# Edge counting in groups of 125 edges and 12 targets, four groups to a PSUM bank

## The chip, the cores and the metric

The kernel runs on one core of a Trainium2 chip. The metric is the device time of one execution in microseconds (us); the median of the runs is compared. A core has five engines that work side by side, each with a queue of its own: TensorE (PE, with its weight loads shown apart as PEld), VectorE (DVE), ScalarE (ACT), GpSimd (POOL) and SyncE (SP, which issues most DMAs).

## The reference

The input is `x` (1250 tokens by 1024) and a list of 40,000 edges `src`, `dst`, sorted by `dst`. Two layers of a graph network, then a mixture of experts:

```python
def _sage_layer(h, edge_src, edge_dst, deg_inv, W_self, W_neigh, b):
    msg = h[edge_src]
    agg = jax.ops.segment_sum(msg, edge_dst, num_segments=h.shape[0])
    mean = agg * deg_inv[:, None]
    return h @ W_self + mean @ W_neigh + b
...
h = jax.nn.relu(_sage_layer(x, ..., W_self0, W_neigh0, b0))
out = _sage_layer(h, ..., W_self1, W_neigh1, b1)
...
x = x + gnn(layernorm(x), src, dst, ...)
x = x + ffn(layernorm(x), ...)     # router, two of eight experts a token
```

All in float32. The targets are drawn so that low numbers get many more edges than high ones: `dst` is 1250 times the square of a uniform number.

## The kernel before

The kernel doesn't gather messages. It builds a matrix `C` of counts once (source by target, 10 blocks of 128 sources by 1250 targets) and multiplies with it: the sum over the edges becomes a product, in both layers.

**How counts are made.** The edges, in order of target, are cut into groups of 250 (`EG`), each of two chunks of 125 (`GC`, `GP`). Two groups make a row of groups; there are `R` = 80 rows. The targets of a group lie close together, so the group counts into a window of `WIN` = 24 targets that begins at its own base. A source number is taken apart into a high part (its block, 0 to 9) and a low part (its lane, 0 to 127). For each chunk `row_of_groups` makes two one-hot matrices in float16: `ol` on POOL (L409, edge by lane, 128 wide) and `oh` on DVE (L416, edge by block and window place, `NB * WIN` = 240 wide). A matmul of the two (L419) counts the edges of the chunk by lane, block and window place, and the two chunks of a group add up in PSUM. The two groups of a row share one PSUM bank (`cnt`, three buffers).

**How they get into `C`.** Two rows of groups are left open. Then `close_row` takes the oldest: for each of its groups it loads the base from SBUF into a register of DVE (`values_load`, L433) and adds the window to `C` at this place (L438, 128 x 240 float32). `oh` and `ol` have six buffers each (pool `hot`).

**What comes ahead of it.** `make_keys` works out, for every edge, its place in the window (block times `WIN` plus target minus base) and its lane, with edges in rows of 500; `turn_keys` brings them into the layout of one edge a partition by transposes, and `turn_ranges` the bases and the least and greatest target of each group into one row. `verdict` tests on DVE whether every group fits its window. If not (`plain` is 0), the kernel runs a general path at its end. The general path isn't run for these inputs.

**What the order is.** The first steps are in an order written by hand (L467 to L495). After that the instructions are placed by the scheduler of the framework, by program order and by its estimate of when each is ready; on each engine the order is then fixed. The program mixes the rows of groups with the products of the first layer: 9 rows around the first of them, then 10 rows for each 128 columns of the rest of `W_self0` (`self_unit`, L458, two or four rows to a unit), then one row to each of the ten `y_unit`s of the first quarter of `W_neigh0` (L524), and the last row after these. When all rows are closed, a product with ones sums `C` over the sources (L549) and gives the degrees; then the first product with `C` follows (L560). So nothing after L549 can begin before the last add of L438. The rest of the kernel (second layer, router, experts) doesn't touch what is changed here.

Of the kernel before, what the change touches and what calls it, by code (L numbers as in the profile page):

```python
# [10 lines left out]
F32 = mybir.dt.float32  # L11
F32R = mybir.dt.float32r
F16 = mybir.dt.float16
# [3 lines left out]
ALU = mybir.AluOpType  # L17
AX = mybir.AxisListType
# [2 lines left out]

P = 128
EPS = 1e-5
WIN = 24
GC, GP = 2, 125


@with_exitstack
def kernel(
# [21 lines left out]
    nc = tc.nc  # L51
    N, D = x.shape
    NE = src.shape[0]
# [4 lines left out]
    QW = D // 4  # L58
    NB = -(-N // P)
    NP = NB * P  # L60
    EG = GC * GP
    NGR = NE // EG
    R = NGR // 2
    WEXP = KD * H + KH * D
    NTILE = (2 * N) // P + E
    assert R * 2 * EG == NE and R <= P and 2 * NB * WIN <= 512 and N > WIN
    rows = [min(P, N - b * P) for b in range(NB)]

    step = -(-(N - 2 * P) // 4) * 2
# [3 lines left out]
    def blk(b):  # L73
        return slice(b * P, b * P + rows[b])
# [4 lines left out]
    const = ctx.enter_context(tc.tile_pool(name="const", bufs=1))  # L79
# [11 lines left out]
    L = land.tile([P, NT + 4 * D + 2 * WQ], F32, name="L")  # L91
# [4 lines left out]
    def row_of(i):  # L96
        return SC[:, (i % 4) * D : (i % 4 + 1) * D]
# [7 lines left out]
    def load_q(w, q):  # L105

        t = WW[:, turn[0] * WQ : (turn[0] + 1) * WQ].rearrange("p (k n) -> p k n", k=KD)
        turn[0] ^= 1
        tc.keep_in_program_order(
            nc.sync.dma_start(  # L110
                out=t, in_=w[:, q * QW : (q + 1) * QW].rearrange("(k p) n -> p k n", p=P)
            )
        )
        return t
# [27 lines left out]
    stt = nc.vector.scalar_tensor_tensor  # L142


    RE = 2 * EG
    assert 8 * RE <= 4000 and 3 * NGR <= 500 and 8480 + 6 * NGR <= 9440
    edge = L[:R, 4000:8000].rearrange("p (a n) -> p a n", n=RE)
    dst_i, src_i, hi_i, lo_i = (edge[:, a, :].bitcast(I32) for a in range(4))
    dst_f, hi_f, lo_f, key = (edge[:, a, :] for a in range(4, 8))
    for b in range(2):  # L150
        for h, eng in enumerate((nc.sync, nc.scalar)):
            hs = slice(h * HALF, (h + 1) * HALF)
            eng.dma_start(out=row_of(b)[: rows[b], hs], in_=x[blk(b), hs])
    nc.sync.dma_start(out=dst_i, in_=dst.rearrange("(g n) -> g n", n=RE))
    nc.scalar.dma_start(out=src_i, in_=src.rearrange("(g n) -> g n", n=RE))
    ws_first = load_q(w_self0, 0)
# [9 lines left out]
    ident = const.tile([P, P], F32, name="ident")  # L166
# [22 lines left out]
    lane = counted(iota([P, P], [[1, P]]), "lane", F16)  # L189
# [6 lines left out]
    nc.scalar.dma_start(out=b0_p, in_=b0.rearrange("(k p) -> p k", p=P))  # L196


    ext = const.tile([R, 3, 2], F32, name="ext")
    base_i = const.tile([1, NGR], I32, name="base_i")  # L200

    keys = const.tile([GP, 2, 2 * GC, R], F32, name="keys")
    worst = const.tile([1, 1], F32, name="worst")
    plain = const.tile([1, 1], I32, name="plain")
    gx = L[:1, 8000 : 8000 + 3 * NGR].rearrange("o (a g) -> o a g", a=3)
    lo_, hi_ = gx[:, 0, :], gx[:, 1, :]
    APART = 16
    assert APART * EG < 4096

    dst_halves = dst_f.rearrange("p (a n) -> p a n", a=2)  # L210

    def make_keys():

        nc.vector.tensor_reduce(ext[:, 0, :], dst_halves, AX.X, ALU.min)
        nc.vector.tensor_scalar(ext[:, 2, :], ext[:, 0, :], float(N - WIN), None, op0=ALU.min)
        nc.vector.tensor_scalar(hi_i, src_i, 7, None, op0=ALU.arith_shift_right)
        nc.vector.tensor_scalar(lo_i, src_i, P - 1, None, op0=ALU.bitwise_and)
        nc.vector.tensor_copy(hi_f, hi_i)
        nc.vector.tensor_copy(lo_f, lo_i)
        stt(key, hi_f, float(WIN), dst_f, op0=ALU.mult, op1=ALU.add)  # L220
        for i in range(2):
            part = key[:, i * EG : (i + 1) * EG]
            nc.vector.tensor_scalar(part, part, ext[:, 2, i : i + 1], None, op0=ALU.subtract)

    def turn_keys():
        for a, v in enumerate((key, lo_f)):
            ps = tpp.tile([P, 4, P], F32, name="tp")
            pf = ps.rearrange("p a b -> p (a b)")
            for c in range(2 * GC):
                nc.tensor.transpose(  # L230
                    pf[:GP, c * R : (c + 1) * R], v[:, c * GP : (c + 1) * GP], ident[:R, :R]
                )
            nc.scalar.copy(keys[:, a].rearrange("p c g -> p (c g)"), pf[:GP, : 2 * GC * R])

    def turn_ranges():

        nc.vector.tensor_reduce(ext[:, 1, :], dst_halves, AX.X, ALU.max)
        for a in (2, 0, 1):
            pe = tpp.tile([P, 4, P], F32, name="tp")
            for i in range(2):  # L240
                nc.tensor.transpose(pe[:1, i, :R], ext[:, a, i : i + 1], ident[:R, :R])
            nc.vector.tensor_copy(
                gx[:, a, :].rearrange("o (r i) -> o i r", i=2), pe[:1, :2, :R]
            )
            if a == 2:
                nc.vector.tensor_copy(base_i, gx[:, 2, :])

    def verdict():

        bad = L[:1, 8480 : 8480 + 6 * NGR].rearrange("o (a g) -> o a g", a=6)  # L250
        nc.vector.memset(bad, -1.0)
        stt(bad[:, 0, :], hi_, float(1 - WIN), lo_, op0=ALU.add, op1=ALU.subtract)
        nc.vector.tensor_tensor(bad[:, 1, : NGR - 1], lo_[:, : NGR - 1], lo_[:, 1:], ALU.subtract)
        nc.vector.tensor_tensor(bad[:, 2, : NGR - 1], hi_[:, : NGR - 1], hi_[:, 1:], ALU.subtract)
        stt(
            bad[:, 3, : NGR - APART], hi_[:, : NGR - APART], 1.0, lo_[:, APART:],
            op0=ALU.add, op1=ALU.subtract,
        )
        nc.vector.tensor_scalar(bad[:, 4, :], hi_, float(1 - N), None, op0=ALU.add)
        nc.vector.tensor_scalar(bad[:, 5, :], lo_, -1.0, None, op0=ALU.mult)  # L260
        nc.vector.tensor_reduce(worst, bad.rearrange("o a g -> o (a g)"), AX.X, ALU.max)
        nc.vector.tensor_scalar(plain, worst, 0.0, None, op0=ALU.is_le)
# [90 lines left out]
    def gnn_windows():  # L353
# [6 lines left out]
        pc = pcs.enter_context(tc.tile_pool(name="pc", bufs=3, space=PSUM))  # L360
# [18 lines left out]
        hot = y0.enter_context(tc.tile_pool(name="hot", bufs=6, side="right"))  # L379

        yh = yp.tile([P, NB, QW], F32R, name="yh")
        yl = yp.tile([P, NB, QW], F32R, name="yl")
        win = yp.tile([P, NB * WIN], F16, name="win")
        win_i = yp.tile([P, NB * WIN], I32, name="win_i")
        nc.gpsimd.iota(win_i, pattern=[[1, NB * WIN]], base=0, channel_multiplier=0)
# [18 lines left out]
        GW = NB * WIN  # L404

        def row_of_groups(r):
            ol = hot.tile([GP, 2 * GC, P], F16, name="ol")
            for c in range(2 * GC):
                nc.gpsimd.tensor_scalar(  # L409
                    ol[:, c, :], lane[:GP], keys[:, 1, c, r : r + 1], None, op0=ALU.is_equal  # L410
                )
            ps = pc.tile([P, 2, 256], F32, name="cnt")
            for i in range(2):
                for c in range(GC):
                    oh = hot.tile([GP, GW], F16, name="oh")
                    nc.vector.tensor_scalar(  # L416
                        oh, win[:GP], keys[:, 0, i * GC + c, r : r + 1], None, op0=ALU.is_equal
                    )
                    nc.tensor.matmul(  # L419
                        ps[:, i, :GW], ol[:, i * GC + c, :], oh,  # L420
                        start=(c == 0), stop=(c == GC - 1),
                    )
            open_rows.append((r, ps))
            if len(open_rows) > 2:
                close_row()
# [2 lines left out]

        def close_row():
            r, ps = open_rows.pop(0)  # L430
            for i in range(2):
                g = 2 * r + i
                at = nc.values_load(  # L433
                    base_i[0:1, g : g + 1], engines=(ENG.DVE,), min_val=0, max_val=N - WIN,
                    skip_runtime_bounds_check_because="cut at N - WIN, and a target is never below 0",
                )
                to = C[:, :, ds(at, WIN)]
                nc.vector.tensor_tensor(  # L438
                    to, to.bitcast(F32),
                    ps[:, i, :GW].rearrange("p (k w) -> p k w", k=NB), ALU.add,  # L440
                )
# [64 lines left out]
        some_groups(2)  # L506
        self_unit(ws_first, 1, 2)
        verdict()
        for q in range(1, 4):
            w_q = w_next  # L510
# [21 lines left out]
        for q in range(4):  # L532
# [8 lines left out]
            if q == 0:  # L541
# [4 lines left out]
                for c0, n in cchunks:  # L546
                    ps = mm.tile([P, 512], F32, name="ps")
                    for k in range(NB):
                        nc.tensor.matmul(  # L549
                            ps[:, :n], ones_r, C[:, k, c0 : c0 + n],  # L550
                            start=(k == 0), stop=(k == NB - 1),
# [3 lines left out]
            for c0, n in cchunks:  # L555
                for d in (2 * q, 2 * q + 1):
                    ps = mm.tile([P, 512], F32, name="ps")
                    for k in range(NB):
                        for part in (yh, yl):
# [3 lines left out]
                                start=(k == 0 and part is yh), stop=(k == NB - 1 and part is yl),  # L563
# [1093 lines left out]
```

## Time and profile before

| | us |
|---|---|
| three runs | 1163.17, 1163.0, 1160.78 |
| median | 1163.0 |
| the profiled execution, its own time | 1160.5 |
| its span, first to last instruction | 1158.6 |
| first one-hot on POOL (L409) | 32.2 |
| last add into `C` (L438) begins | 234.2 |
| column sums (L549) begin | 234.6 |

The mean granted TensorE clock is 0.993. Times in the profile are counted from the first instruction of the span. In a line of a group stand the source line, engine, operation, what it writes and reads, the shape and the number of instructions; then their busy time in us, the mean of one in ns, and the idle time of the engine just before them with what ended it. In the table by stages each engine has its busy time and the number of instructions; the last three columns are the granted clock, the share of DMA and GB/s. `DVEq` is DVE's sequencer, which loads registers and works out addresses; its instructions count as no busy time.

### The profile page before, as it was taken

How to read it: one execution, taken by the hardware profiler on the slowest of the kernel's cores; microseconds unless marked ns; L12 is line 12 of the kernel's file. 1: busy time of each engine (PE TensorE's matmuls, PEld its weight loads, DVE VectorE, ACT ScalarE, POOL GpSimd, SP SyncE). 2: the span in 40 equal slices, each digit the busy share in tenths (PEclk: the TensorE clock that was granted, in tenths of full speed). 3: DMA queues.
4: the chain of work that ended last, by engine and by line, in shares of the span. 5: the costliest groups of instructions: out<-in, count | busy, mean ns of one | idle time of the engine just before them, and what ended most of it. 6: DMA issues, size and time to landing. Idle time of an engine off the chain costs nothing.

```text
span 1158.6 us, 13209 instructions
## 1 busy us (share of the span) xinstructions
PE 1122.4 (97%) x4775; PEld 789.3 (68%) x4775; DVE 452.2 (39%) x1127; ACT 181.5 (16%) x420; POOL 331.3 (29%) x438
## 2 busy tenths in 40 slices
PE   6999999999999999999999999999999989999994
PEld 4556556888888886887788688865333666666662
DVE  8767778751212164241234142555221532111110
ACT  5301000001111111100110000122111223222220
POOL 1899999700000000031004011540000013323221
PEclk9999999999999999999999999999999999999997
DMA  7011011010100021042014432347801435554542
GB/s 230 32 40 39 1 37 37 1 37 1 37 1 1 1 73 37 10 170 72 1 34 164 167 118 73 145 164 257 279 19 36 146 89 132 107 121 101 126 116 45
DMA packets 59330, 95.40 MB, mean 82 GB/s; under 512 B 8797, under 2 KB 35645, under 8 KB 59251
## 3 DMA queue, kind: packets, MB, share of 16 engines
q1 hardware_dynamic: 48400, 67.72, 17.0%
q0 software_dynamic: 7056, 23.88, 9.1%
q10 hardware_dynamic: 3798, 2.84, 0.8%
q8 instruction: 42, 0.69, 0.2%
q14 instruction: 34, 0.28, 0.1%
HBM read 68.76 MB, written 27.47 MB: 83 GB/s over the span
## 4 chain that ended last, share of the span: by engine, by line
PE 94%; DVE 2%; ACT 1%; DMA 1%; POOL 1%; issue 0%; ACTq 0%; DVEq 0%; POOLq 0%
PE ps L524 12%; PE ps L458 11%; PE psb L638 9%; PE ps L708 8%; PE ps L560 8%; PE ps L638 7%; PE ps L1493 7%; PE ps L1518 7%; PE ps L1173 5%; PE ps L625 5%; PE ps L1186 4%; PE cnt L419 3%; PE ps L1128 2%; PE tp L1481 2%; PE lg L1105 2%; PE ps L1514 1%
## 5 line engine op out<-in xcount | busy, mean ns | idle before, releaser
L409 POOL TENSOR_SCALAR ol<-lane,keys 125x128 f16<-125x128 f16 x320 | 192.1, 619 | 27.7 <-DVE oh L416 27.7
L458 PE MATMUL ps<-h0T,L 128*128 128x498 f32 (+2 forms) x384 | 147.6, 517 | 0.3 <-ACT h0T L321 0.2
L524 PE MATMUL ps<-L,h0T 128*128 128x256 f32 (+1 forms) x640 | 142.2, 379 | 0.0
L704 POOL TENSOR_TENSOR L<-L 128x512 f32<-128x512 f32 (+1 forms) x20 | 32.0, 1608 | 375.6 <-DVE L L617 217.6
L524 PEld LDWEIGHTS ps<-L,h0T 128*128 128x128 f32 (+1 forms) x640 | 118.3, 187 | 18.0 <-issue 0.6
L416 DVE TENSOR_SCALAR oh<-win,keys 125x240 f16<-125x240 f16 x320 | 85.7, 322 | 30.9 <-PE cnt L419 29.1
L458 PEld LDWEIGHTS ps<-h0T,L 128*128 128x128 f32 x384 | 67.5, 192 | 39.0 <-issue 33.9
L1493 PE MATMUL ps<-xw,L 128*128 x368 | 84.7, 383 | 0.3 <-issue 0.3
L1518 PE MATMUL ps<-xw,L 128*128 x184 | 83.5, 596 | 0.1
L560 PE MATMUL ps<-C,yh 128*128 128x256 f32 (+2 forms) x240 | 81.8, 356 | 0.0
L560 PE MATMUL ps<-C,yl 128*128 128x256 f32 (+2 forms) x240 | 81.5, 353 | 0.0
L708 PE MATMUL ps<-zh,C 128*128 128x512 f32 (+1 forms) x200 | 79.5, 398 | 0.0
L708 PE MATMUL ps<-zl,C 128*128 128x512 f32 (+1 forms) x200 | 78.6, 393 | 0.0
L1493 PEld LDWEIGHTS ps<-xw,L 128*128 128x128 f32 x368 | 69.0, 192 | 10.1 <-issue 1.4
L1529 POOL DMA_INDIRECT out_dram<-L x23 | 36.3, 1579 | 133.4 <-ACT L L1482 87.9
L1470 POOL DMA_INDIRECT L<-t_d,L x26 | 26.0, 1000 | 162.2 <-DVE L L140 142.2
L438 DVE TENSOR_TENSOR C<-C,cnt 128x240 f32 x160 | 64.4, 402 | 13.4 <-DVE oh L416 2.1
L1518 PEld LDWEIGHTS ps<-xw,L 128*128 128x128 f32 x184 | 33.2, 190 | 35.3 <-issue 33.0
L140 DVE TENSOR_TENSOR L<-L,ps 128x512 f32<-128x512 f32 (+1 forms) x28 | 17.1, 611 | 99.7 <-PE ps L1173 47.2
L419 PEld LDWEIGHTS <-ol 125*128 125x128 f16 x320 | 31.0, 97 | 36.6 <-POOL ol L409 21.7
L419 PE MATMUL cnt<-oh,ol 125*128 125x240 f16 x320 | 50.8, 265 | 2.5 <-POOL ol L409 2.1
L1526 DVE TENSOR_SCALAR L<-ps,L 128x512 f32<-128x512 f32 x23 | 17.3, 751 | 91.7 <-PE ps L1518 91.7
(224 smaller groups left out, 1516.6 us busy)
## 6 DMA issues: line engine op xcount, KB each, us to landing
xw<-in_L_ffn_ew_dram SPq DMA_DIRECT2D x16, 1024.0 KB, 7.6
L<-in_x_dram SPq DMA_DIRECT2D x20, 256.0 KB, 2.9
v_d<-L SPq DMA_DIRECT2D x18, 256.0 KB, 2.0
xa<-v_d SPq DMA_DIRECT2D x18, 256.0 KB, 5.9
t_d<-L SPq DMA_DIRECT2D x9, 512.0 KB, 4.4
out_dram<-xa SPq DMA_DIRECT2D x9, 512.0 KB, 4.0
L<-in_L_gnn_W_self_dram SPq DMA_DIRECT2D x4, 1024.0 KB, 5.7
L<-in_L_gnn_W_neigh_dram SPq DMA_DIRECT2D x4, 1024.0 KB
```

The lines of the kernel that those rows point to most:

```text
L409: nc.gpsimd.tensor_scalar(ol[:, c, :], lane[:GP], keys[:, 1, c, r : r + 1], None, op0=ALU.is_equal)
L416: nc.vector.tensor_scalar(oh, win[:GP], keys[:, 0, i * GC + c, r : r + 1], None, op0=ALU.is_equal)
L419: nc.tensor.matmul(ps[:, i, :GW], ol[:, i * GC + c, :], oh, start=(c == 0), stop=(c == GC - 1),)
L438: nc.vector.tensor_tensor(to, to.bitcast(F32), ps[:, i, :GW].rearrange("p (k w) -> p k w", k=NB), ALU.add,)
L458: nc.tensor.matmul(ps[:, :n], w[:, k, (d % 2) * P : (d % 2 + 1) * P], h0T[:, k, c0 : c0 + n], start=(k == 0), stop=(k == KD - 1),)
L524: nc.tensor.matmul(ps[:m, :QW], hT[:, k, blk(b)], w[:, k, :], start=(k == 0), stop=(k == KD - 1))
L560: nc.tensor.matmul(ps[:, :n], part[: rows[k], k, (d % 2) * P : (d % 2 + 1) * P], C[: rows[k], k, c0 : c0 + n], start=(k == 0 and part is y ...
L625: nc.tensor.matmul(ps[:m], hT1[:, k, blk(b)], w[:, k, :], start=(k == 0), stop=(k == KD - 1))
L638: nc.tensor.matmul(ps, rows_of(k), w[:, k, :], start=(first and k == 0), stop=(k == KB - 1), skip_group_check=not first,)
L708: nc.tensor.matmul(ps[:m], C[: rows[k], k, blk(b)], part[: rows[k], k, :], start=(k == 0 and part is yh), stop=(k == NB - 1 and part is yl),)
L1493: nc.tensor.matmul(ps[:, :H], xT[:, k, :], w1_all[:, ds(e, 1), k * H : (k + 1) * H], start=(k == 0), stop=(k == KD - 1),)
L1518: nc.tensor.matmul(ps, hT[:, q, :], w2_all[:, ds(e, 1), q * D + h * HALF : q * D + (h + 1) * HALF], start=False, stop=(q == KH - 1),)
```

## The change

The groups become half as long and their windows half as wide: 125 edges (`EG`) and 12 targets. Each chunk is now a group of its own, so there are 320 groups, four (`RG`) to a row and to a PSUM bank, and still 80 rows. The number of `ol`, `oh` and matmul instructions stays 320 each; `oh` and the moving side of the matmul go from 240 to 120 columns. No two matmuls add up in PSUM any more. `close_row` adds four windows of 120 instead of two of 240, each with a register load of its own. Key and range tables, the test of the windows and the scratch space that these use are sized for 320 groups; the scratch of `verdict` moves to where the edge numbers stood.

```diff
--- before.py
+++ after.py
@@ -21,8 +21,9 @@
 
 P = 128
 EPS = 1e-5
-WIN = 24
-GC, GP = 2, 125
+WIN = 12
+EG = 125
+RG = 4
 
 
 @with_exitstack
@@ -58,12 +59,11 @@
     QW = D // 4
     NB = -(-N // P)
     NP = NB * P
-    EG = GC * GP
     NGR = NE // EG
-    R = NGR // 2
+    R = NGR // RG
     WEXP = KD * H + KH * D
     NTILE = (2 * N) // P + E
-    assert R * 2 * EG == NE and R <= P and 2 * NB * WIN <= 512 and N > WIN
+    assert R * RG * EG == NE and R <= P and RG * NB * WIN <= 512 and N > WIN
     rows = [min(P, N - b * P) for b in range(NB)]
 
     step = -(-(N - 2 * P) // 4) * 2
@@ -142,8 +142,8 @@
     stt = nc.vector.scalar_tensor_tensor
 
 
-    RE = 2 * EG
-    assert 8 * RE <= 4000 and 3 * NGR <= 500 and 8480 + 6 * NGR <= 9440
+    RE = RG * EG
+    assert 8 * RE <= 4000 and 3 * NGR <= 1440 and 6 * NGR <= 4 * RE
     edge = L[:R, 4000:8000].rearrange("p (a n) -> p a n", n=RE)
     dst_i, src_i, hi_i, lo_i = (edge[:, a, :].bitcast(I32) for a in range(4))
     dst_f, hi_f, lo_f, key = (edge[:, a, :] for a in range(4, 8))
@@ -196,29 +196,29 @@
     nc.scalar.dma_start(out=b0_p, in_=b0.rearrange("(k p) -> p k", p=P))
 
 
-    ext = const.tile([R, 3, 2], F32, name="ext")
+    ext = const.tile([R, 3, RG], F32, name="ext")
     base_i = const.tile([1, NGR], I32, name="base_i")
 
-    keys = const.tile([GP, 2, 2 * GC, R], F32, name="keys")
+    keys = const.tile([EG, 2, RG, R], F32, name="keys")
     worst = const.tile([1, 1], F32, name="worst")
     plain = const.tile([1, 1], I32, name="plain")
     gx = L[:1, 8000 : 8000 + 3 * NGR].rearrange("o (a g) -> o a g", a=3)
     lo_, hi_ = gx[:, 0, :], gx[:, 1, :]
-    APART = 16
+    APART = 32
     assert APART * EG < 4096
 
-    dst_halves = dst_f.rearrange("p (a n) -> p a n", a=2)
+    dst_groups = dst_f.rearrange("p (a n) -> p a n", a=RG)
 
     def make_keys():
 
-        nc.vector.tensor_reduce(ext[:, 0, :], dst_halves, AX.X, ALU.min)
+        nc.vector.tensor_reduce(ext[:, 0, :], dst_groups, AX.X, ALU.min)
         nc.vector.tensor_scalar(ext[:, 2, :], ext[:, 0, :], float(N - WIN), None, op0=ALU.min)
         nc.vector.tensor_scalar(hi_i, src_i, 7, None, op0=ALU.arith_shift_right)
         nc.vector.tensor_scalar(lo_i, src_i, P - 1, None, op0=ALU.bitwise_and)
         nc.vector.tensor_copy(hi_f, hi_i)
         nc.vector.tensor_copy(lo_f, lo_i)
         stt(key, hi_f, float(WIN), dst_f, op0=ALU.mult, op1=ALU.add)
-        for i in range(2):
+        for i in range(RG):
             part = key[:, i * EG : (i + 1) * EG]
             nc.vector.tensor_scalar(part, part, ext[:, 2, i : i + 1], None, op0=ALU.subtract)
 
@@ -226,28 +226,28 @@
         for a, v in enumerate((key, lo_f)):
             ps = tpp.tile([P, 4, P], F32, name="tp")
             pf = ps.rearrange("p a b -> p (a b)")
-            for c in range(2 * GC):
+            for c in range(RG):
                 nc.tensor.transpose(
-                    pf[:GP, c * R : (c + 1) * R], v[:, c * GP : (c + 1) * GP], ident[:R, :R]
-                )
-            nc.scalar.copy(keys[:, a].rearrange("p c g -> p (c g)"), pf[:GP, : 2 * GC * R])
+                    pf[:EG, c * R : (c + 1) * R], v[:, c * EG : (c + 1) * EG], ident[:R, :R]
+                )
+            nc.scalar.copy(keys[:, a].rearrange("p c g -> p (c g)"), pf[:EG, : RG * R])
 
     def turn_ranges():
 
-        nc.vector.tensor_reduce(ext[:, 1, :], dst_halves, AX.X, ALU.max)
+        nc.vector.tensor_reduce(ext[:, 1, :], dst_groups, AX.X, ALU.max)
         for a in (2, 0, 1):
             pe = tpp.tile([P, 4, P], F32, name="tp")
-            for i in range(2):
+            for i in range(RG):
                 nc.tensor.transpose(pe[:1, i, :R], ext[:, a, i : i + 1], ident[:R, :R])
             nc.vector.tensor_copy(
-                gx[:, a, :].rearrange("o (r i) -> o i r", i=2), pe[:1, :2, :R]
+                gx[:, a, :].rearrange("o (r i) -> o i r", i=RG), pe[:1, :, :R]
             )
             if a == 2:
                 nc.vector.tensor_copy(base_i, gx[:, 2, :])
 
     def verdict():
 
-        bad = L[:1, 8480 : 8480 + 6 * NGR].rearrange("o (a g) -> o a g", a=6)
+        bad = L[:1, 4000 : 4000 + 6 * NGR].rearrange("o (a g) -> o a g", a=6)
         nc.vector.memset(bad, -1.0)
         stt(bad[:, 0, :], hi_, float(1 - WIN), lo_, op0=ALU.add, op1=ALU.subtract)
         nc.vector.tensor_tensor(bad[:, 1, : NGR - 1], lo_[:, : NGR - 1], lo_[:, 1:], ALU.subtract)
@@ -404,22 +404,18 @@
         GW = NB * WIN
 
         def row_of_groups(r):
-            ol = hot.tile([GP, 2 * GC, P], F16, name="ol")
-            for c in range(2 * GC):
+            ol = hot.tile([EG, RG, P], F16, name="ol")
+            for i in range(RG):
                 nc.gpsimd.tensor_scalar(
-                    ol[:, c, :], lane[:GP], keys[:, 1, c, r : r + 1], None, op0=ALU.is_equal
-                )
-            ps = pc.tile([P, 2, 256], F32, name="cnt")
-            for i in range(2):
-                for c in range(GC):
-                    oh = hot.tile([GP, GW], F16, name="oh")
-                    nc.vector.tensor_scalar(
-                        oh, win[:GP], keys[:, 0, i * GC + c, r : r + 1], None, op0=ALU.is_equal
-                    )
-                    nc.tensor.matmul(
-                        ps[:, i, :GW], ol[:, i * GC + c, :], oh,
-                        start=(c == 0), stop=(c == GC - 1),
-                    )
+                    ol[:, i, :], lane[:EG], keys[:, 1, i, r : r + 1], None, op0=ALU.is_equal
+                )
+            ps = pc.tile([P, RG, P], F32, name="cnt")
+            for i in range(RG):
+                oh = hot.tile([EG, GW], F16, name="oh")
+                nc.vector.tensor_scalar(
+                    oh, win[:EG], keys[:, 0, i, r : r + 1], None, op0=ALU.is_equal
+                )
+                nc.tensor.matmul(ps[:, i, :GW], ol[:, i, :], oh, start=True, stop=True)
             open_rows.append((r, ps))
             if len(open_rows) > 2:
                 close_row()
@@ -428,8 +424,8 @@
 
         def close_row():
             r, ps = open_rows.pop(0)
-            for i in range(2):
-                g = 2 * r + i
+            for i in range(RG):
+                g = RG * r + i
                 at = nc.values_load(
                     base_i[0:1, g : g + 1], engines=(ENG.DVE,), min_val=0, max_val=N - WIN,
                     skip_runtime_bounds_check_because="cut at N - WIN, and a target is never below 0",
```

## The prediction

> **What bounds the kernel now.** I read the page first, then the table by stages, then the lines that the change edits, last the order of time around the end of the counting.
>
> ```profile
> span 1158.6 us, 13209 instructions
> PE 1122.4 (97%) x4775; PEld 789.3 (68%) x4775; DVE 452.2 (39%) x1127; ACT 181.5 (16%) x420; POOL 331.3 (29%) x438
> ...
> L409 POOL TENSOR_SCALAR ol<-lane,keys 125x128 f16<-125x128 f16 x320 | 192.1, 619 | 27.7 <-DVE oh L416 27.7
> ...
> L416 DVE TENSOR_SCALAR oh<-win,keys 125x240 f16<-125x240 f16 x320 | 85.7, 322 | 30.9 <-PE cnt L419 29.1
> ...
> L438 DVE TENSOR_TENSOR C<-C,cnt 128x240 f32 x160 | 64.4, 402 | 13.4 <-DVE oh L416 2.1
> ...
> L419 PE MATMUL cnt<-oh,ol 125*128 125x240 f16 x320 | 50.8, 265 | 2.5 <-POOL ol L409 2.1
> ```
>
> Over the whole span TensorE (PE) is the bound. That average hides the only stage that the change touches, the counting of edges, from about 32 to 235 us. The stage table (engines PE, PEld, DVE, ACT, POOL) and the two queue rows of the add:
>
> ```profile
> 66.00:105.00 39.00, 38.88 (x165) 22.70 (x164) 29.45 (x109) 3.65 (x6) 39.00 (x66) 1.00 0.14 30
> 105.00:192.00 87.00, 87.00 (x350) 48.73 (x349) 68.97 (x237) 7.57 (x13) 87.00 (x148) 1.00 0.08 26
> ...
> L433 DVEq TENSOR_LOAD <-base_i x160: 297/303/548, 37.7 to 233.7; - x160
> ...
> L438 DVEq FUSED_REGOPS  x160: 69/69/69, 38.4 to 234.1; - x160
> ```
>
> The reader should see three engines near their limit at once: PE and POOL show 87.00 of 87 us, VectorE (DVE) 69. And DVE's figure leaves out its queue: each of the 160 adds has a register load of 303 ns and an address computation of 69 ns, which count as no busy time. The end of the stage in order of time:
>
> ```profile
> 118.45 0.93 DVE L438 TENSOR_TENSOR C<-C,cnt 128x240 f32 x2 [0.23 <-DVE oh L416]
> 119.29 1.24 DVE L416 TENSOR_SCALAR oh<-win,keys 125x240 f16<-125x240 f16 x4
> ...
> 214.88 9.44 POOL L409 TENSOR_SCALAR ol<-lane,keys 125x128 f16<-125x128 f16 x16
> ...
> 225.66 0.85 DVE L416 TENSOR_SCALAR oh<-win,keys 125x240 f16<-125x240 f16 x4
> ...
> 232.46 0.57 PE L419 MATMUL cnt<-oh,ol 125*128 125x240 f16 x4
> ...
> 233.65 0.93 DVE L438 TENSOR_TENSOR C<-C,cnt 128x240 f32 x2 [0.16 <-DVE yl L390]
> 234.63 5.58 PEld L549 LDWEIGHTS ps<-C,ones_r 128*128 128x128 f32 x30 [1.87 <-DVE C L438]
> ```
>
> POOL's last one-hot ends at 214.88 + 9.44 = 224.3. PE reaches the last row of groups at 232.5, because float32 products stand ahead of it; the last add ends at 234.6 and releases the column sums. All later work needs the finished counts, so the forecast is where that 234.6 moves to.
>
> **The change, part by part.**
>
> *TensorE.* Still 320 count matmuls, with 120 columns instead of 240. Four of 240 end 0.57 us after they start and one takes 0.265: (0.57 - 0.265) / 3 = 0.10 us from start to start, 32 us in all. The nearest short row is L1336: 20 matmuls of 69 columns, each with its own weights, in 0.84 us with 0.196 for one, so 0.034 from start to start. By columns, 120 comes to 0.05 and PE saves 320 x 0.05 = 16 us. The Trainium skill ("TensorE: Matmul & The Clock Gate", section Back-to-back issue gap) says that in a stream of weight load and matmul the load counts too, and gives 81 ns a pair at 128 columns; by it PE would save only 320 x 0.02 = 6 us. The L1336 row, with a load for every matmul, speaks for the larger saving, which I take. Either lands on the end only if PE is still last, and POOL allows less.
>
> *POOL.* The 320 `ol` instructions keep their shape: 192.1 us from 32.2 to 224.3, not moved. This is a floor. Behind it the last row still needs its matmuls and, with two rows left open, eight adds at 0.525 (below): 224.5 + 4.2 = 228.7. The most that the change can bring is therefore 234.6 - 228.7, some 6 us.
>
> *VectorE, one-hots.* 320 of 240 columns become 320 of 120. Start to start a run of four takes (0.85 - 0.28) / 3 = 0.19 us with POOL idle (225.66) and (1.24 - 0.3) / 3 = 0.31 with POOL at work (119.29). For half the columns there is no row; bounds are half (0.10-0.16) and unchanged (0.19-0.31). I take 0.15.
>
> *VectorE, adds.* 160 adds of 240 become 320 of 120, and with each comes its load and address: 160 more of these. The datapath alone is mild: the 256 and 498 column rows of the same operation (0.422 and 0.676) give 1.05 ns a column, hence 0.28 us for 120: 320 x 0.28 = 90 us against 64. The Trainium skill ("VectorE: DVE Perf Modes", section The TRN2 errata) speaks against cutting tiles small because each instruction pays a fixed part; its formula, 120 cycles and one a column at 0.96 GHz, gives 0.25 us for 120, 80 us in all, and 20 us more than before by the same formula. The trace has a dearer row: two adds that follow each other end 0.93 after they start, each taking 0.405, so they start 0.525 apart. That is longer than the add itself; the gap is load, address and issue (303 + 69 + about 150 ns between them). This doesn't shrink with the width. By the rule a row of groups costs DVE 4 x 0.15 + 4 x 0.25 = 1.6 us and it stays ahead of POOL's 2.4 (4 x 0.6): the change would be a gain. By the row it is 4 x 0.525 = 2.1 us for the adds alone, against 2 x 0.525 now. The measured row decides.
>
> *The VectorE chain, summed.* In each row stand four one-hots and then four adds. The one-hots (0.6 us) run partly under the first load (0.3): 2.1 + 0.3 = 2.4 us a row. If all of them hide it is 2.1, if none 2.7. From the first add at 38.5, 80 rows: 192 us (168 to 216), to 230.5. Other DVE work from 38 to 234 is now 12 us by its lines (ten `yl` splits 4.2, the verdict, the routing constants and the end of a layernorm 8). The verdict grows by about 3.7: its memset (0.86 at 5.7 us) now lies over the edge numbers, so it must come after the keys and clears twice as much (1.7); the reduction over 1 x 960 (1.14) doubles, and six steps of some 0.3 gain 0.17 each. Of these 16 us half hide behind loads: 8 (0 to 16). Last come waits for PE: `oh` has six buffers, 1.5 rows, and DVE waits 29 us for `cnt` to free one, up to 4.1 us at a time, where PE works through eight float32 products at a stretch. A busier DVE waits less, but doesn't make these stretches shorter, and what it lost there it can no longer catch up: 8 us (0 to 20). Last add: 230.5 + 8 + 8 = 246.5, which is 12 us later than 234.6.
>
> *What is late next.* PE has 16 us less of counting and its float32 products are in hand by then, so it stands and waits for `oh`; that is the cost of the adds becoming the chain. Behind the loads in DVE's queue stand the `oh` of the next row, for which PE waits, and `yl`, which frees the PSUM of the y products.
>
> *The small edits*, together under 1 us: two more subtractions in `make_keys` (0.33 for 250 columns now, about 0.16 for 125, so +0.1, and the keys are ready well before the transposes at 30.3, which wait behind PE's products); six more transposes of one column in `turn_ranges` (0.07 apart); four copies of 320 instead of 160 (+0.17 each, before the first load). If the cover of the products is gone, they cost that 1 us. The DMAs of edges and weights keep their number and place. One PSUM bank for each row and three rows of buffers stay.
>
> The sum for the profiled execution: 1160.5 (span 1158.6 and 1.9 around it) + 12 = 1172.5. The median of the three runs shown, 1163.0, stands 2.5 above that execution; so 1175 in its terms. A measurement of this kernel tells about 0.2%, 2.3 us, from no change.
>
> **The rivals.**
>
> 1. *POOL stays the slowest* (chance 0.13). If loads run under the one-hots and the queue runs far enough ahead, DVE needs 2.1 us a row, POOL 2.4, and PE, lighter by 16 us, has all products done when POOL ends. Then the end is 228.7 and the time 1163 - 6 = 1157. For it: stretches in which DVE was behind show adds 0.43 apart (`0.83` for two), so the load can hide at times. Against: these have one load to hide and not four, and a queue can't hide more than its own sum, already 168 us.
>
> 2. *The two cancel* (chance 0.09). 2.2 to 2.3 us a row with waits of 5 us: the last add falls at 232 to 237, 1161 to 1165.
>
> 3. *The register load becomes the chain* (chance 0.78, my forecast). It decides from the point where a row on DVE, loads included, is longer than POOL's 2.4 us: 0.3 us a row beyond it is 24 us. By its bounds the shift goes from nothing to 254.5 + 16 + 20 - 234.6 = 56 us; all three terms at their ends together is unlikely, two of them give about 34.
>
> 4. *The change doesn't do what it says*: a group of 125 with more than 12 targets would send everything through the general path and nearly double the time. Worked out from the reference's targets, the widest group of 125 spans 10 (the widest of 250 spans 18 of 24). I leave it out.
>
> **How the numbers follow.** The forecast is case 3's 1175. The range goes down to 1158, which takes in case 2 and nearly all of case 1, and up to 1163 + 34 = 1197. Faster is case 1 with a little of case 2's lower edge; same is the rest of case 2 and case 3's lower edge.
>
> **What would show it.** Right: 320 `TENSOR_LOAD` of about 303 ns, adds near 0.28 us but still about 0.52 apart in runs of four; waits of PE's loads for `oh` instead of `ol`; POOL with gaps late in the stage, as it waits for `ol` buffers; the first L549 at about 247; everything from there to the end as long as now, 924 us. Wrong: L549 before 232 with POOL still busy without a gap (case 1); count matmuls 0.08 apart (the rule on weight loads was right); adds 0.3 apart (the load hides, and the forecast falls).

## The result, and the profile after

The changed kernel takes 1212.4 us (median of 4 runs, 1208.6 to 1213.1), the kernel before 1162.2 beside it: a ratio of 1.043 (95% interval 1.040 to 1.045), 50 us slower. The forecast was 1175 with a range up to 1197: the direction was right, the size was not, and the range missed it.

The profiled execution took 1211.7 (span 1209.8). Lines of its page, in the order of those shown of before; the changed lines have other numbers now (`oh` L415, matmul L418, register load L429, add L434, first-layer products L454, y products L520, column sums L545):

```profile
span 1209.8 us, 13697 instructions
...
L409 POOL TENSOR_SCALAR ol<-lane,keys 125x128 f16<-125x128 f16 x320 | 190.2, 612 | 68.9 <-PE cnt L418 41.8
...
L434 DVE TENSOR_TENSOR C<-C,cnt 128x120 f32 x320 | 89.2, 279 | 60.2 <-DVE C L434 51.5
...
L418 PE MATMUL cnt<-oh,ol 125*128 125x120 f16 x320 | 44.8, 232 | 38.4 <-DVE oh L415 37.3
L415 DVE TENSOR_SCALAR oh<-win,keys 125x120 f16<-125x120 f16 x320 | 69.3, 278 | 27.8 <-PE cnt L418 26.6
```

The reader should see three engines waiting for each other. The matmuls waited 37 us for `oh` from DVE; DVE waited 27 us for matmuls to free `oh` and 51.5 behind its own adds; POOL, which never waited for PE before, waited 41.8. A ring like this has no single slow engine; one has to ask *when* each wait happens. The table by stages (PE, PEld, DVE, ACT, POOL; then granted clock, DMA share, GB/s):

```profile
66.00:105.00 39.00, 39.00 (x150) 21.25 (x148) 22.23 (x92) 4.12 (x7) 28.97 (x50) 1.00 0.10 15
105.00:192.00 87.00, 83.58 (x325) 48.15 (x324) 49.52 (x219) 7.94 (x14) 59.04 (x102) 0.96 0.11 37
192.00:234.00 42.00, 14.55 (x72) 7.41 (x72) 32.27 (x145) 0.00 (x0) 42.00 (x72) 0.51 0.00 1
234.00:290.00 56.00, 38.93 (x191) 31.05 (x191) 35.54 (x143) 2.60 (x7) 25.76 (x44) 0.75 0.06 20
```

From 66 to 192 PE is nearly full, while from 105 on POOL has 59 of 87 us where it had 87, and DVE 49.5 where it had 69. In these 87 us POOL waits 29.4 for PE; DVE waits 14.7 for PE and 18.0 behind its own adds. From 192 to 234 it is the other way round: PE has 14.6 of 42, only count matmuls, and the granted clock falls to 0.51. Before the change PE was full there too:

```profile
192.00:234.00 42.00, 41.03 (x223) 34.02 (x221) 30.35 (x101) 4.12 (x11) 32.31 (x55) 1.00 0.08 27
```

The work that could have filled this stretch was done in the one ahead of it. PE's order of time shows it, first of before, then of after:

```profile
143.16 0.57 PE L419 MATMUL cnt<-oh,ol 125*128 125x240 f16 x4
143.57 1.84 PE L458 MATMUL ps<-h0T,L 128*128 128x496 f32 x4
145.24 0.57 PE L419 MATMUL cnt<-oh,ol 125*128 125x240 f16 x4
```

```profile
114.01 0.38 PE L418 MATMUL cnt<-oh,ol 125*128 125x120 f16 x4
114.22 2.72 PE L454 MATMUL ps<-h0T,L 128*128 128x496 f32 x6
116.78 0.22 PE L418 MATMUL cnt<-oh,ol 125*128 125x120 f16 x1
116.83 1.05 PE L454 MATMUL ps<-h0T,L 128*128 128x496 f32 x2
117.72 0.32 PE L418 MATMUL cnt<-oh,ol 125*128 125x120 f16 x3
```

Here, before, four passes of a float32 product stand between two rows of groups (two products of two passes each, 1.67 us). After, eight do (2.56 + 0.89 = 3.45 us), six of them ahead of the row and two inside it. These are typical places; counted from row 9 to row 46 (rows counted from 0), PE does 5.2 passes a row before and 9.0 after. The scheduler lays this order once, by its estimate of when a row is ready. The changed rows came 127.2 / 37 = 3.4 us apart, although DVE can do one in 2.3, as it shows when PE has nothing else:

```profile
207.06 0.88 DVE L415 TENSOR_SCALAR oh<-win,keys 125x120 f16<-125x120 f16 x4
207.86 0.58 DVE L434 TENSOR_TENSOR C<-C,cnt 128x120 f32 x2
208.67 0.28 DVE L434 TENSOR_TENSOR C<-C,cnt 128x120 f32 x1 [0.23 <-DVE C L434]
209.19 0.28 DVE L434 TENSOR_TENSOR C<-C,cnt 128x120 f32 x1 [0.24 <-DVE C L434]
209.39 0.84 DVE L415 TENSOR_SCALAR oh<-win,keys 125x120 f16<-125x120 f16 x4
```

This is a row from 207.06 to 209.39. In it stand both of the forecast's prices: an add of 0.28 us, and 0.52 from add to add.

Where the 50.4 us lie, by the times at which the count matmuls of a row begin (rows counted from 0):

| | before | after | difference |
|---|---|---|---|
| row 9 begins | 66.4 | 63.6 | -2.8 |
| row 9 to row 46 | 83.8 | 127.2 | +43.4 |
| row 46 to row 69 | 53.3 | 53.8 | +0.5 |
| row 69 to row 79 | 29.0 | 34.1 | +5.1 |
| row 79 to the column sums | 2.1 | 6.3 | +4.2 |
| column sums begin | 234.6 | 285.0 | +50.4 |

From there to the end it is 924.8 us against 924.0. Nearly all of the loss lies in rows 9 to 46, the stretch in which PE is full; 2.9 us of it are a wait of PE for a load of weights (`W_self0`).

### The profile page after: what moved, and what is told of

It is laid out like the page before. It is cut to its first block, busy times and chain, and to the rows that moved or that the text cites. A ratio compares the mean times of both kernels' runs of the same rounds, so it can differ in the third digit from the quotient of the medians.

```text
span 1209.8 us, 13697 instructions
## 1 busy us (share of the span) xinstructions
PE 1128.3 (93%) x4781; PEld 791.3 (65%) x4781; DVE 463.1 (38%) x1289; ACT 181.4 (15%) x420; POOL 326.9 (27%) x438
## 4 chain that ended last, share of the span: by engine, by line
PE 89%; DVE 5%; ACT 1%; DMA 1%; issue 1%; DVEq 1%; POOL 1%; ACTq 0%; POOLq 0%
PE ps L520 12%; PE ps L454 11%; PE psb L634 9%; PE ps L704 8%; PE ps L556 8%; PE ps L634 7%; PE ps L1489 6%; PE ps L1514 6%; PE ps L1169 5%; PE ps L621 5%; PE ps L1182 4%; DVE C L434 2%; PE ps L1124 2%; PE tp L1477 2%; PE lg L1101 2%
## 5 line engine op out<-in xcount | busy, mean ns | idle before, releaser
L409 POOL TENSOR_SCALAR ol<-lane,keys 125x128 f16<-125x128 f16 x320 | 190.2, 612 | 68.9 <-PE cnt L418 41.8
L454 PE MATMUL ps<-h0T,L 128*128 128x498 f32 (+2 forms) x384 | 149.0, 530 | 3.3 <-DMA L<-in_L_gnn_W_self_dram 2.9
L520 PE MATMUL ps<-L,h0T 128*128 128x256 f32 (+1 forms) x640 | 143.4, 384 | 1.6 <-DVE yl L390 1.6
L520 PEld LDWEIGHTS ps<-L,h0T 128*128 128x128 f32 (+1 forms) x640 | 120.5, 190 | 20.0 <-DVE yl L390 2.0
L434 DVE TENSOR_TENSOR C<-C,cnt 128x120 f32 x320 | 89.2, 279 | 60.2 <-DVE C L434 51.5
L454 PEld LDWEIGHTS ps<-h0T,L 128*128 128x128 f32 x384 | 69.7, 195 | 46.4 <-issue 41.9
L418 PE MATMUL cnt<-oh,ol 125*128 125x120 f16 x320 | 44.8, 232 | 38.4 <-DVE oh L415 37.3
L415 DVE TENSOR_SCALAR oh<-win,keys 125x120 f16<-125x120 f16 x320 | 69.3, 278 | 27.8 <-PE cnt L418 26.6
L418 PEld LDWEIGHTS <-ol 125*128 125x128 f16 x320 | 28.4, 102 | 72.8 <-POOL ol L409 45.2
```

The lines of the kernel that those rows point to most:

```text
L409: nc.gpsimd.tensor_scalar(ol[:, i, :], lane[:EG], keys[:, 1, i, r : r + 1], None, op0=ALU.is_equal)
L415: nc.vector.tensor_scalar(oh, win[:EG], keys[:, 0, i, r : r + 1], None, op0=ALU.is_equal)
L418: nc.tensor.matmul(ps[:, i, :GW], ol[:, i, :], oh, start=True, stop=True)
L434: nc.vector.tensor_tensor(to, to.bitcast(F32), ps[:, i, :GW].rearrange("p (k w) -> p k w", k=NB), ALU.add,)
L454: nc.tensor.matmul(ps[:, :n], w[:, k, (d % 2) * P : (d % 2 + 1) * P], h0T[:, k, c0 : c0 + n], start=(k == 0), stop=(k == KD - 1),)
L520: nc.tensor.matmul(ps[:m, :QW], hT[:, k, blk(b)], w[:, k, :], start=(k == 0), stop=(k == KD - 1))
```

## The experiments

Two explanations: **order** (the scheduler takes a row for dearer than it is, spreads the rows on PE, and thereby holds DVE and POOL back) and **chain** (DVE really can't do a row faster beside the others). The runs of before beside these had medians of 1161.1 to 1161.6.

**1. The changed kernel with the stage in an order by hand.**

```diff
+        man.enter_context(tc.manual_schedule(engines={ENG.DVE, ENG.Activation, ENG.PE}))
...
+        def product_done(us):
+            credit[0] += us
+            if credit[0] >= PACE:        # 2.1
+                credit[0] -= PACE
+                some_groups(1)
+                if later:
+                    later.pop(0)()       # a split of y, put off to behind a row
```

> The changed kernel, with the instructions of PE, DVE and ACT in the counting stage in an order written out by hand: a row of groups after every 2.1 us of float32 products, the same instructions otherwise. Theory 'order' (the scheduler takes a row of four adds for longer than it is, so it puts three to four products of 0.84 us between two rows and holds DVE and POOL back to 3.5 us a row): rows come about 2.3 us apart through the whole stage, L549 starts near 240, the time is 1160 to 1175. Theory 'chain' (DVE can't do a row in under 3 us when POOL and PE work beside it, whatever the order): rows stay over 3 us apart, 1200 to 1215.

Measured: 1186.5 us, ratio 1.022 (1.020 to 1.023). Half of the loss is gone with the same instructions, so order matters; but it lies between the two forecasts. The rows tell why: row 18 began only at 105.1 (before: 82.8), as the hand order of the first rows is poor, and from there to row 78 a row took (249.4 - 105.1) / 60 = 2.40 us. That is the forecast's 2.4, with POOL and PE at work.

**2. The order by hand from row 9 on only.** The edit is that of run 1 with the block opened ahead of the loop over `q`, and `PACE` 2.2.

> The changed kernel again with PE, DVE and ACT in an order by hand, but only from the tenth row of groups on (the run with the whole stage by hand lost some 20 us before row 18, where the hand order was poor, and then went at 2.40 us a row). Theory 'order' with a real DVE chain of 2.4 us a row: row 10 at 66, 71 rows at 2.4 and two rows of adds at the end, L549 at 240 to 246, time 1166 to 1172. Theory 'chain' with waits of its own: above 1180.

Measured: 1170.8 us, ratio 1.008 (1.006 to 1.010), with the column sums at 242.6. The same instructions in another order on PE, DVE and ACT take 41.6 us less than the changed kernel. What is left is at least in part the chain:

```profile
105.00:192.00 87.00, 86.97 (x381) 51.58 (x380) 64.47 (x290) 8.41 (x15) 85.37 (x144) 1.00 0.11 36
...
DVE C L434 <- DVE C L434: 40.0, 166, 0.6
...
POOL ol L409 <- PE cnt L418: 1.8, 5, 0.5
```

POOL is back at 85.4 of 87 and waits 1.8 us for PE instead of 41.8; DVE still waits 40 us behind its own adds, 0.24 each time, which is the gap between adds that start 0.52 apart; run 5 shows that this gap goes with the register loads. A row takes (233.7 - 86.7) / 60 = 2.45 us from row 18 to row 78. PE is full as well here (86.97 of 87), so the pace of 2.2 us that this order sets can hold a part of that; run 1, at 2.1, took 2.40.

**3. The same kind of order on the kernel before.** The edit of run 2 on before, `PACE` 1.95.

> The kernel before with the same kind of order by hand from the tenth row on (a row after every 1.95 us of products), nothing else changed: what the order by hand is worth without the change. PE has to do all its products and 320 matmuls of 0.10 us; the same order as now in effect: 1158 to 1164. If the order by hand brings an advantage of its own, L549 comes near 229 and the time is 1155 to 1158.

Measured: 1162.7 us, ratio 1.001 (1.000 to 1.002). The order by hand is worth nothing by itself, so run 2 isn't a gain of the hand over the scheduler in general; it undoes a harm. Against this run the changed kernel by hand is 8.1 us slower: the price of the change under these two orders. Their paces differ (2.2 and 1.95 us), and other paces were not run, so the price is not exact.

**4. One register load for the four bases of a row, order by the scheduler.**

```diff
-            for i in range(RG):
-                g = RG * r + i
-                at = nc.values_load(
-                    base_i[0:1, g : g + 1], engines=(ENG.DVE,), ...
+            _, places = nc.values_load_multi_w_load_instructions(
+                base_i[0:1, RG * r : RG * (r + 1)], engines=(ENG.DVE,), ...
+            for i, at in enumerate(places):
```

> The changed kernel, but close_row loads the four bases of a row with one register load instead of four; the order is left to the scheduler. On DVE's queue a row needs one load of 0.30 us and four address computations, so by the row of the trace the adds can follow each other 0.25 to 0.3 us apart and a row takes about 1.8 us. Theory 'order': the planned gaps on PE shrink from 3-4 to 3 products only, since the adds with an address from a register stay priced high; the time falls by some 10 to 25 us only, to 1185-1202. Theory 'loads are all of it' (three loads of 0.5 us a row on DVE's queue): the time falls to the POOL floor, 1155 to 1163.

Measured: 1179.0 us, ratio 1.015 (1.013 to 1.017), 33 us less than the changed kernel, more than theory 'order' gave it and far from the floor. PE's order now mostly has six passes between rows:

```profile
109.18 0.37 PE L418 MATMUL cnt<-oh,ol 125*128 125x120 f16 x4
109.39 2.72 PE L454 MATMUL ps<-h0T,L 128*128 128x498 f32 x6
111.95 0.38 PE L418 MATMUL cnt<-oh,ol 125*128 125x120 f16 x4
```

Over rows 9 to 46 PE does 7.6 passes a row instead of 9.0, and a row takes 2.9 us instead of 3.4.

**5. One load for four, and the order by hand from row 9 on.** Runs 2 and 4 together, `PACE` 2.1.

> The changed kernel with one register load for four bases and the same order by hand from the tenth row on. If the loads are what makes the DVE row 2.4 us, DVE needs about 1.8 and POOL's 2.36 to 2.4 us a row is left as the limit: L549 at 228 to 236, time 1154 to 1162. If the adds themselves hold DVE (0.5 us each with or without a load): as the run with four loads, 1166 to 1172.

Measured: 1158.4 us, ratio 0.997 (0.996 to 0.999); column sums at 231.1. That is 12.5 us less than run 2, but the pace differs too (2.1 against 2.2). Run 1 has the pace of 2.1 and all four loads: from row 18 to the column sums it took 258.3 - 105.1 = 153.2 us, this run 231.1 - 85.8 = 145.3. So some 8 us are the loads that are gone; the rest of the 12.5 can be the pace. The row now takes (200.6 - 85.8) / 48 = 2.39 us from row 18 to row 66, which is POOL's pace. One load of four values takes 342 ns, one of a single value 303:

```profile
L427 DVEq TENSOR_LOAD <-base_i x80: 337/342/604, 39.8 to 229.2; - x80
...
152.07 1.22 DVE L434 TENSOR_TENSOR C<-C,cnt 128x120 f32 x4
```

Four adds follow each other (1.22 - 0.28) / 3 = 0.31 us apart, instead of 0.52.

**6. The dear half of the change alone, on before:** groups, windows and one-hots as they were, each add in two halves with a load each.

```diff
-                to = C[:, :, ds(at, WIN)]
+                for h in range(2):
+                    hb = slice(h * NB // 2, (h + 1) * NB // 2)
+                    at = nc.values_load(...)
+                    to = C[:, hb, ds(at, WIN)]
```

> The kernel before, but each add of 240 columns is made as two adds of 120 (blocks 0 to 4, blocks 5 to 9), each with a register load of its own. Groups of 250, windows of 24, one-hots and matmuls as before. It does the dear half of the change alone. If the doubled adds and loads are the whole loss: 1205 to 1220, since nothing gets narrower. If a part of the loss comes from groups and windows (PSUM, keys, verdict): well under that, 1170 to 1190.

Measured: 1217.0 us, ratio 1.048 (1.046 to 1.050). The doubled adds and loads are enough for the whole loss (56 us here, where nothing gets narrower, and 50 in the changed kernel), with the same picture: POOL 58.9 us of the 87 from 105 to 192, then PE 20.7 of 42 at a clock of 0.59.

```profile
105.00:192.00 87.00, 87.00 (x334) 50.49 (x332) 52.48 (x219) 8.35 (x14) 58.91 (x100) 1.00 0.12 37
192.00:234.00 42.00, 20.66 (x90) 11.14 (x89) 32.09 (x138) 0.74 (x2) 40.51 (x69) 0.59 0.00 1
```

**7. The same halves with one load for both.** As run 6, with the load ahead of the loop over `h`.

> The kernel before with each add in two halves of 120 columns that share the register load of their group: 320 adds, 160 loads. Next to the run with 320 loads (1217) it tells adds from loads under the scheduler's order. If the loads are the dear half for planner and chip alike: 1170 to 1185. If the number of adds is: 1200 or more.

Measured: 1176.3 us, ratio 1.012 (1.011 to 1.014). Of the 55 us that run 6 loses, the second loads are 41 and the second adds 15, each with what the scheduler makes of them.

**8. The adds at fixed places,** no register load and no address computation, order by the scheduler.

> The changed kernel with the adds at places fixed in the program instead of loaded bases: no register load and no address computation; the counts then stand in wrong columns, so the output isn't the reference's, the work is otherwise the same. Order left to the scheduler. If it is the price of register-addressed adds that spreads the rows on PE, they now stand as in the program (four rows, then a product of eight; one row before each y product) and POOL's pace with PE's bunches sets the time, as in the run of before with two bases in one load: L549 at 232 to 245, 1160 to 1172. If the rows stay spread by three or four products, the planner's reason is another: 1180 or more.

Measured: 1169.3 us, ratio 1.007 (1.005 to 1.008); column sums at 241.9. Without registers the rows stand on PE as the program has them, and PE meets them before POOL or DVE are ready:

```profile
89.51 0.63 PE L418 MATMUL cnt<-oh,ol 125*128 125x120 f16 x3
90.49 0.23 PE L418 MATMUL cnt<-oh,ol 125*128 125x120 f16 x1 [0.35 <-POOL ol L409]
91.07 0.23 PE L418 MATMUL cnt<-oh,ol 125*128 125x120 f16 x1 [0.35 <-DVE oh L415]
```

So the loads and register addresses, taken together, are what spreads the rows, and a row that is planned too early costs as well.

**9. Two bases in one load, on before.** The edit of run 4 with 2 for `RG`.

> The kernel before, with the two bases of a row in one register load. Theory 'order': the scheduler sees a cheaper row and puts the rows where the program has them, in bunches of six to eight matmuls; DVE then lacks buffers for a bunch, PE waits there, and the end of POOL's 192 us at 224 is the floor: 1153 to 1165. Theory 'loads are all of it': DVE was not the limit before, so nothing changes: 1161 to 1164.

Measured: 1171.8 us, ratio 1.009 (1.008 to 1.011): *slower*, outside both expectations. One load less a row gave a worse kernel. The load of two bases is itself dear:

```profile
L431 DVEq TENSOR_LOAD <-base_i x80: 520/527/775, 37.7 to 243.3; - x80
```

It takes 527 ns where the two loads that it replaces took 303 each, so DVE's queue is relieved by only 0.08 us a row. Why two values take longer than four (342 ns in run 5) stays open. The order got worse: the rows fell back into program order as in run 8, PE waited 5.5 us for POOL on the way, and the y products, each placed behind a row, were late at the end. The last matmuls begin at 242.6, 18.2 us after POOL's last one-hot ends. The floor that I named was not reached, as I had left out that PE's waits in the bunches add to its own work.

**10. Narrowing alone:** before with `WIN` 20 instead of 24.

> The kernel before with windows of 20 targets instead of 24 and nothing else (the widest group spans 18): narrowing alone, without more groups. Count matmuls 0.083 apart instead of 0.10 (5 us of PE over 320), one-hots and adds a sixth shorter, no new instruction. POOL's floor leaves at most 6 us: 1156 to 1162 if the order stays as good as it is; 1163 to 1172 if a cheaper row makes the scheduler put rows earlier than POOL has them, as with two bases in one load.

Measured: 1159.9 us, ratio 0.998 (0.998 to 0.999), 2 us faster. Narrower windows do help when they bring no more instructions.

**11. The y products ahead of the rows,** in the changed kernel (`tc.high_priority()` around `y_unit`), because PE had done three of them by 191 and the fourth only by 253.

> The changed kernel, scheduler's order, with the ten y products given priority over the rows of groups, so that they no longer wait behind the adds in DVE's order (in the changed kernel PE has three y products done at 191 and the fourth only at 253). If the held y products are a large part of the loss: 1185 or less. By the table of rows they cost only the stretch of 3.7 us a row at the end, 8 rows x 1.4 = 11 us: 1198 to 1206.

Measured: 1224.7 us, ratio 1.054 (1.052 to 1.056): slower, a miss. Done earlier, the y products only held the rows back more: row 54 came at 226.8 instead of 209.7, and from there rows went at 2.34 us with PE nearly empty. Column sums at 291.7; another 8 us come after them, which I didn't follow up. So moving the y products up doesn't win the loss back; their late place goes with the same bad share-out.

**12. The best version that these runs point to:** run 5 with one of the four `ol` of a row on DVE, `PACE` 1.94.

```diff
-                nc.gpsimd.tensor_scalar(
+                (nc.vector if i == 3 else nc.gpsimd).tensor_scalar(
                     ol[:, i, :], lane[:EG], keys[:, 1, i, r : r + 1], None, op0=ALU.is_equal
```

> The changed kernel with one load for four bases, an order by hand with a row after every 1.94 us of products, and one of the four lane one-hots of a row made on DVE instead of POOL. POOL then needs 1.8 us a row, DVE about 2.0, PE 2.15; if nothing else holds them PE is the limit again and has 16 us less to do than before: L549 at 218 to 228, time 1144 to 1156. If POOL or DVE slow each other down, or DVE comes out over 2.3 us a row: 1158 or more.

Measured: 1153.3 us, ratio 0.993 (0.991 to 0.994), faster than both kernels; column sums at 224.1.

```profile
105.00:192.00 87.00, 86.97 (x392) 51.31 (x391) 76.86 (x361) 8.43 (x15) 71.27 (x119) 1.00 0.11 37
```

PE is full and POOL has slack (71.3 of 87): PE is the limit again, a row takes (165.1 - 84.9) / 36 = 2.23 us, and the cheaper count matmuls reach the end at last.

## Why the prediction was right and wrong

**Prices.** They held. Count matmuls come (0.38 - 0.22) / 3 = 0.05 us apart in their runs of four, so the short row of before was the right guide here, and not the 81 ns a pair of the Trainium skill ("TensorE: Matmul & The Clock Gate", section Back-to-back issue gap). The add takes 0.28 us and the next starts 0.52 later. A row on DVE took 2.33 us with PE out of products, and rows in an order by hand came 2.40 to 2.45 apart, forecast 2.4. That the register load outweighs the add was right, and so was the choice of the queue's row over the formula of the Trainium skill ("VectorE: DVE Perf Modes", section The TRN2 errata), by which the estimate for an add was 0.25 us and nothing for its load.

**The step that failed** is the last term of the VectorE chain, "waits for PE: 8 (0 to 20)", and with it the step on what is late next, by which PE "stands and waits for `oh`". Both took PE's order as given, with more room in it. In truth the order is made anew for the changed program, and it answered the dearer adds with 9.0 passes a row instead of 5.2. So at first it was DVE and POOL that waited for PE, and rows 9 to 46 took 43 us longer; PE waited for `oh` only afterwards, when its products were used up. The sign for this is POOL: the prediction expected its gaps late in the stage, and they came early (59 of 87 us busy from 105 to 192, 42 of 42 from 192 to 234). The bounds of the term on waits didn't contain the 43 us, since they were read from waits under the old order. With the order put right (run 2), the forecast's own sum is close: 1170.8 measured, 1175 forecast, column sums at 242.6 and not 247. In part this agreement is made by the run itself: its pace, 2.2 us of products and 0.2 of counting, comes to the forecast's 2.4 us a row.

**The range.** The bounds of the prediction came to a shift of 56 us, 1219 in its terms, and were cut to 34 as what two terms at their ends give. That sum is wrong: the chain at its end with one of the other two gives 12 + 24 + 8 = 44 or 12 + 24 + 12 = 48; only the other two together give 32. The wider range would have held 1212 by luck, since what grew was the distance between rows in PE's order, not DVE's own row. At the lower end, 1158 leaves out the 1157 of the prediction's own first rival.

**What could have been seen.** Before the change, the scheduler's share-out was already visible: up to about 107 us rows stand mostly in bunches as in the program, from there to about 200 mostly one after each four passes. Rows spread over products by an estimate were a sign that a dearer row would be spread more. I read the pattern as a fact of the kernel rather than as an answer to its costs.

**The rivals.** The POOL floor (1157) isn't what the change does, but it is what the same groups do once the loads are out of the way and the order is level (run 5: 1158.4). Why the scheduler spaces the rows as it does can't be read from a trace. Counted from row 9 to row 46, its spacing goes with loads and register-addressed adds, but not with the number of loads alone: one load of four values (run 4) spread the rows more than two loads of one (run 7).

| kernel, order by the scheduler | loads a row | adds a row | passes a row | us |
|---|---|---|---|---|
| before | 2 | 2 | 5.2 | 1162.2 |
| run 9, before | 1 of two values | 2 | 4.8 | 1171.8 |
| run 7, before | 2 | 4 | 6.1 | 1176.3 |
| run 6, before | 4 | 4 | 9.1 | 1217.0 |
| changed | 4 | 4 | 9.0 | 1212.4 |
| run 4, changed | 1 of four values | 4 | 7.6 | 1179.0 |
| run 8, changed | none | 4, at fixed places | 4.8 | 1169.3 |

The orders by hand moved PE, DVE and ACT together; which engine's order did the harm was not tested apart.

## What to carry to other kernels

Count the queue's instructions of each piece, above all register loads, before cutting it into more pieces: here 160 more loads and adds cost more than 16 us of saved matmul time, and fetching several values with one load took most of that back. Where a scheduler lays the order, an edit changes two things, the work and the order. Compare the order of the engine that runs out of work (what stands between two of its dependent pieces, before and after), and try the new work in an order with even gaps before judging it. A cheaper piece can also get a worse order, so measure after every step.

## What the runs showed that I had not expected

- The granted TensorE clock fell to 0.51 from 192 to 234 us, where PE had nothing but 72 count matmuls. The first full y product after it took 5.13 us at a clock of 0.71, the next one 3.68 at 1.00:

```profile
248.29 5.13 PE L520 MATMUL ps<-L,h0T 128*128 128x256 f32 x16
253.47 3.68 PE L520 MATMUL ps<-L,h0T 128*128 128x256 f32 x16
```

The column sums, behind a last stretch of count matmuls alone, took 7.66 us at a clock of 0.76 instead of 6.00 at 1.00. So the products that followed such stretches ran slower, too.

- One register load of four neighbouring values takes 342 ns, of one value 303, of two 527.
- Loading two bases at once made the kernel before 0.9% slower (run 9): it saved 0.08 us of loads a row and got a worse order.
